# A diagonal LSTM and a small quantum circuit: late statistics in pieces of columns, state tiles reused as row buffers, new rows' states set by Pool

## The chip, the cores and the metric

One NeuronCore of one Trainium2 chip. The metric is device time in microseconds of the one core, and the time of a kernel is the median of its runs. A profile is of one execution; times inside it are in microseconds from the first instruction.

## The reference

The input `x` is 16 images of 128 channels, 64 rows and 64 columns, in float32. Two layers follow each other, each with a group norm ahead of it (32 groups of 4 channels) and a residual sum behind it.

Layer 0 is a diagonal LSTM. Row r is shifted right by r columns, so that 127 steps run over diagonals; a step takes all 64 rows at once:

```
i_s = w_is @ skew(gn(x)) + b_is
gates = i_s[t] + w_ss0 @ (h of the row above) + w_ss1 @ h + b_ss
o, f, i = sigmoid(gates[:384]);  g = tanh(gates[384:])
c = f * c + i * g;   h = o * tanh(c)
x1 = x + unskew(h)
```

A row's state also moves ahead of its first column: outside the image the input is zero, and the state that a row has reached when its first column comes depends on the row alone, not on the image.

Layer 1 works on each pixel: `gn(x1)` is projected to 4 angles, a fixed circuit of 4 qubits is simulated, its 4 expectation values are projected back to 128 channels, and `x1` is added. The group norm between the layers needs mean and variance of every group over all rows and columns of `x1`, so layer 1 can start only when the last column of the last row is there.

## The kernel before

**Tiling.** Channels are the 128 partitions. The 64 rows run in two bands of 32 slots. Slot s holds row s in band 0 and row 32 + s in band 1, which starts 65 steps later (`BAND`), so there are 160 steps (`NSTEP`). A step's columns are 16 images for each active slot, kept as two halves q (even and odd slots), up to 256 columns each. The window of active columns grows over the first 32 steps, is full to about step 128, and shrinks to the end (`columns`, `active`).

**Memory.** `ring` holds 40 of the 64 rows of all images; it is where x is read and where x1 is written. When a block of 4 rows of rows 0 to 23 is finished, SP writes it to a DRAM buffer `low` and loads rows 40 to 63 in its place. `spare` are four buffers of 512 columns. `hst` are two state buffers (read in one step, written in the next), `xns` two buffers of normalised input; both come from a pool of the scan.

**A step** (`step(t, ps)`, lines 736 to 844) is written out by hand for each engine, in program order:

- PE: products of the state with the recurrent weights into the gates' PSUM (line 745; with few columns `w1T` and `w0T` straight on the state, otherwise `wsT` on half 0, then both on differences), then the next step's input products (`gate_ps`, line 585).
- DVE: a difference of halves (line 604), `statistics(n)` (line 699), the sums of halves in PSUM for each gate (line 760), then `c * f` (806), `i * g` (812), the sum (815) and `h = tanh(c) * o` for each half (825).
- ACT: copies of a half (792), four gate activations (764), tanh (816).
- Pool: differences (607, 610), `residual(t - 1)`, which adds h to x in `ring` (619), `normalised(t + 2)` (566, 571, 576), and the group norm's late sums.

After line 825 come the states of rows that begin. `begin(copy, v, s, of, r)` copies row r's starting state, one column of `hinv` or `cinv`, to the 16 columns of slot s (line 600): for h on DVE, after the half q that the slot is in; for c on ACT. Starting states of rows from 33 on are computed inside the scan itself: in the first 32 steps one extra column rides behind the window (`reach`), and `waits` (line 721 on DVE; 727, 730 and 734 on Pool) moves it on.

**Statistics of the second group norm.** When the last row of a block of 4 rows is finished, `residual` puts (block, image) pairs into `waiting`, and each step takes 4 or 6 of them: `bn_stats` of 256 columns each, on DVE. Blocks 0 to 7 are summed in the middle of the scan (`early_sums`), which gives a provisional `mean2`. Each later block's deviations from it are added up on Pool as the block comes (`late_sums`). Four images of the last two blocks are instead summed on ACT (`by_scalar`, with `accum_out`). After the last step come the last residual, 12 `bn_stats` of the last block, 8 passes on ACT, the deviations, and a chain of small matmuls that sum over groups of channels (line 872), between which `fill` keeps PE busy. The mean and the variance lead to `rstd2` and to weights for each image.

**Layer 1** (lines 921 to 1054) runs over images: `angles` (950), `sines`, `squares` (978), `outputs` (996), `finish` (1013), which adds b and x1 and issues the store on SP (1015). Rows 0 to 23 of an image come back from `low` in three chunks, by Pool's DMA (`load`, line 848), through 14 buffers: the four `spare` and ten of a pool that takes the scan's memory. The four `spare` are loaded eight steps ahead of the scan's end, by SP; the other ten loads are issued after the scan.

## Time and profile before

| | |
|---|---|
| median of 3 runs | 1428.9 us (1428.24 to 1432.19) |
| profiled execution | 1429.22 us, span 1427.4 us |
| mean granted PE clock | 0.996 |
| PE busy | 1368.5 us (96%) |
| DVE busy | 973.7 us (68%) |
| ACT busy | 785.3 us (55%) |
| Pool busy | 903.7 us (63%) |
| moved by DMA | 107.05 MB |
| first gate activation | 105.9 us |
| last state written | 1285.1 us |
| first store issued | 1302.5 us |

A group's line of the profile reads: line, engine, operation, output<-input, shape, count, then busy time and length, and in brackets the engine's idle time ahead of it with what ended it. In the slices each digit is a fortieth of the span, in tenths busy. A busy PE is not PE at its peak: matmuls are pipelined and their ends are modelled. Times of Pool are rough.

### The profile page before, as it was taken

Reading aid. Unit: us, or ns where it says so; the run is one execution under the profiler, and the core shown is the slowest. Engines: PE = TensorE matmul, PEld = TensorE weight load, DVE = VectorE, ACT = ScalarE, POOL = GpSimd, SP = SyncE. Lnnn points to the kernel's source line nnn. Section 1 sums busy time; section 2 is a strip of 40 time slices with the busy share of each in tenths; the row PEclk is TensorE's granted clock in tenths of the full one; section 3 lists DMA queues with packets and bytes.
Section 4 is the critical chain, followed back from the end, with each engine's and each line's share of the span. In section 5 each row is a group of like instructions: output and inputs, shape, how many; then the busy total and the mean of one; then the engine's idle time right before and its main releaser. Section 6 shows DMA issues by size and latency. Waiting matters only on the chain. (4 is left out here: it accounts for less than half of the span.)

```text
span 1427.4 us, 20012 instructions
## 1 busy us (share of the span) xinstructions
PE 1368.5 (96%) x5984; PEld 967.6 (68%) x5984; DVE 973.7 (68%) x2438; ACT 785.3 (55%) x1888; POOL 903.7 (63%) x1747
## 2 busy tenths in 40 slices
PE   6778999999999999999999999999999999988898
PEld 5658887777766777667667777766777777883232
DVE  7984566566665666887777776555555578777877
ACT  4555666555555555555555555555555566555231
POOL 3225777777766677788878877766666667642120
PEclk9999999999999999999999999999999999999999
DMA  9970000000000000133333100000000000106999
GB/s 325 369 275 1 1 1 1 1 0 1 1 0 1 1 0 1 60 118 119 118 118 118 60 1 1 1 1 0 1 1 1 1 1 1 31 2 217 359 365 326
DMA packets 87756, 107.05 MB, mean 75 GB/s; under 512 B 5424, under 2 KB 72016, under 8 KB 87648
## 3 DMA queue, kind: packets, MB, share of 16 engines
q1 hardware_dynamic: 82688, 93.34, 19.1%
q0 software_dynamic: 3728, 11.62, 2.5%
q8 instruction: 48, 0.79, 0.2%
q10 hardware_dynamic: 1232, 0.80, 0.2%
q14 instruction: 60, 0.49, 0.1%
HBM read 59.61 MB, written 46.14 MB: 74 GB/s over the span
## 5 line engine op out<-in xcount | busy, mean ns | idle before, releaser
L585 PE MATMUL ps<-xn,wxT 128*128 128x512 f32 (+18 forms) x1280 | 481.3, 519 | 1.7 <-POOL xn L576 1.7
L760 DVE TENSOR_TENSOR ps<-ps,both 128x256 f32<-128x256 f32 (+9 forms) x544 | 221.1, 408 | 315.4 <-PE ps L745 306.2
L764 ACT ACTIVATE ps<-ps,bias 128x512 f32<-128x512 f32 (+23 forms) x480 | 279.2, 583 | 220.8 <-DVE ps L760 184.6
L585 PEld LDWEIGHTS ps<-xn,wxT 128*128 128x128 f32 x1280 | 232.5, 192 | 174.2 <-issue 155.5
L745 PE MATMUL ps<-spare,w1T 128*128 128x256 f32 (+14 forms) x1088 | 305.5, 362 | 0.0
L745 PE MATMUL ps<-spare,w0T 128*128 128x256 f32 (+14 forms) x1088 | 305.5, 362 | 0.0
L792 ACT COPY both<-ps 128x256 f32<-128x256 f32 (+9 forms) x544 | 191.6, 355 | 178.3 <-PE ps L745 158.8
L619 POOL TENSOR_TENSOR ring<-ring,hst 128x256 f32<-128x256 f32 (+8 forms) x488 | 247.9, 540 | 21.0 <-DVE hst L825 21.0
L745 PEld LDWEIGHTS ps<-hst,wsT 128*128 128x128 f32 x1088 | 195.8, 190 | 85.6 <-DVE hst L825 36.7
L745 PE MATMUL ps<-hst,wsT 128*128 128x256 f32 (+14 forms) x1088 | 241.4, 365 | 5.4 <-DVE hst L825 4.1
L745 PEld LDWEIGHTS ps<-spare,w0T 128*128 128x128 f32 x1088 | 201.1, 190 | 21.2
L745 PEld LDWEIGHTS ps<-spare,w1T 128*128 128x128 f32 x1088 | 201.0, 190 | 21.1
L576 POOL TENSOR_TENSOR xn<-xn,rstd 128x512 f32<-128x512 f32 (+10 forms) x160 | 170.8, 1067 | 12.5
L571 POOL TENSOR_TENSOR xn<-ring 128x256 f32<-128x256 f32 (+8 forms) x213 | 147.0, 700 | 0.0
L825 DVE TENSOR_TENSOR hst<-g,ps 128x256 f32<-128x256 f32 (+13 forms) x320 | 107.8, 368 | 45.2 <-ACT g L816 42.7
L816 ACT ACTIVATE g<-cst 128x256 f32<-128x256 f32 (+20 forms) x320 | 103.0, 368 | 64.3 <-DVE cst L815 63.5
L566 POOL TENSOR_TENSOR xn<-ring,mean 128x16 f32<-128x16 f32 (+8 forms) x247 | 130.9, 540 | 7.5 <-DVE mean L143 6.1
L610 POOL TENSOR_TENSOR spare<-hst 128x240 f32<-128x240 f32 (+9 forms) x136 | 103.1, 758 | 35.5 <-DVE hst L825 31.6
L764 ACT ACTIVATE g<-ps,bias 128x512 f32<-128x512 f32 (+20 forms) x160 | 97.3, 608 | 28.4 <-DVE ps L760 22.2
L843 POOL COPY spare<-hst 128x16 f32<-128x16 f32 x64 | 25.1, 392 | 134.2 <-DVE hst L825 134.2
L815 DVE TENSOR_TENSOR cst<-cst,ps 128x256 f32<-128x256 f32 (+20 forms) x320 | 104.4, 368 | 5.5
L812 DVE TENSOR_TENSOR ps<-ps,g 128x512 f32<-128x512 f32 (+20 forms) x160 | 95.1, 594 | 17.7 <-ACT g L764 17.3
(355 smaller groups left out, 1244.0 us busy)
## 6 DMA issues: line engine op xcount, KB each, us to landing
ring<-in_x_dram SPq DMA_DIRECT2D x80, 256.0 KB, 5.6
out_dram<-ring SPq DMA_DIRECT2D x80, 256.0 KB, 5.0
low<-ring SPq DMA_DIRECT2D x6, 2048.0 KB, 7.8
ring<-in_x_dram SPq DMA_DIRECT2D x6, 2048.0 KB, 8.0
low<-low POOLq DMA_DIRECT2D x32, 256.0 KB, 5.6
out_dram<-low SPq DMA_DIRECT2D x32, 256.0 KB, 5.0
spare<-in_x_dram SPq DMA_DIRECT2D x27, 256.0 KB, 5.5
rest<-in_x_dram SPq DMA_DIRECT2D x21, 256.0 KB, 5.6
```

Of the source, the lines that this page charges most:

```text
L566: nc.gpsimd.tensor_sub(by_pairs(xn, 0, j, n), x0, over(mean1, n))
L571: nc.gpsimd.tensor_sub(by_pairs(xn, 1, j, n), lower, of)
L576: nc.gpsimd.tensor_mul(v, v, r)
L585: nc.tensor.matmul(ps[g][:, :, a:b], lhsT=wxT[:, g * 128 : (g + 1) * 128], rhs=xns[t % 2][:, :, a:b], start=t > 0, stop=True, skip_group_c ...
L610: nc.gpsimd.tensor_sub(diff[:, 0, a1:b], now[:, 1, a1 - NB : b - NB], now[:, 0, a1:b])
L619: nc.gpsimd.tensor_add(x1, x1, by_pairs(new, q, j, n))
L745: nc.tensor.matmul(out, lhsT=w[:, g * 128 : (g + 1) * 128], rhs=rhs, start=False, stop=True, skip_group_check=True,)
L760: nc.vector.tensor_add(v, v, both[g][:, a:b])
L764: nc.scalar.activation(to[:, :, a:w], ps[g][:, :, a:w], FUNC[g], bias=bias[:, g : g + 1])
L792: nc.scalar.copy(both[g][:, a:b], ps[g][:, 0, a:b])
L815: nc.vector.tensor_add(c[:, q], c[:, q], ig[:, q])
L825: nc.vector.tensor_mul(new[:, q, a:v], th[:, q, a:v], act[GO][:, q, a:v])
```

## The change

1. **Statistics by pieces.** Blocks 8 to 13 are taken in two halves of columns (0 to 31, 32 to 63), each as soon as it is finished in all four rows; block 14 in 48 and 16 columns; block 15 in 48 and 12 columns. `statistics` takes a budget in microseconds of estimated work (0.12 plus 0.0035 a column) where it took a count. Pieces' deviations are scaled by the piece's share, one more instruction on Pool for each, and `late_sums` runs for each piece.
2. **A last strip.** The last 4 columns of block 15, all images at once, are done after the last step: a subtraction of `mean2`, a square and two sums. The passes on ACT (`by_scalar`) and the DVE deviations of the last block go. In the last three steps a second call of `statistics` stands ahead of the last gate's sum. Two fills fewer stand among the matmuls.
3. **State tiles.** `xns` and `hst` are now `spare` 4 to 7. At the scan's end SP loads low rows 4, 5 and 7 into them in the last two steps, and row buffer 6 after the last residual. The pool of other low buffers has six instead of ten.
4. **New rows' states.** In band 0 a new row's h is copied by Pool, early in the step, not by DVE at its end, and the multiplication of the odd half leaves these columns out where they are its last. In band 1 the copy stays on DVE, behind both halves. `waits` writes both halves' extra column with one instruction.
5. **Fills of the sums.** `added` and `inner` are zeroed and `by_one` is made at step 32 rather than ahead of step 0; `sums_of` and `less` go.

The changed kernel's order on the engines, where the diff alone does not tell it: on Pool, two runs of `late_sums` and the issue of the first load of the pool's six buffers stand ahead of the last residual. The numbers of pieces by step are 9 and 7 in steps 101 and 102, and so on every four steps to 122; 9, 7 in 133, 134 and 137, 138; then 9, 8, 7, 5, 6, 7, 6 in steps 141 to 147, 5 to 7 in steps 148 to 155, none in 156, and 11, 11 and 10 in the last three.

The diff, cut to its core:

```diff
-    spare = [const.tile([P, CHUNK], F32, name=f"spare{i}") for i in range(4)]
+    spare = [const.tile([P, CHUNK], F32, name=f"spare{i}") for i in range(8)]
...
-        hst = [state.tile([P, 2, NC], F32, name=f"hst{i}") for i in range(2)]
-        xns = [state.tile([P, 2, NC], F32, name=f"xn{i}") for i in range(2)]
+        xns, hst = ([v.rearrange("p (q n) -> p q n", q=2) for v in spare[i : i + 2]] for i in (4, 6))
...
-                if t == 4 * g + 3 + (NW - 1 if 4 * g < SLOTS else BAND + NW - 1 - SLOTS):
-                    n = NB - LATE if g >= NG2 - 2 else NB
-                    waiting.extend((g, i) for i in range(n))
+                done = t - (4 * g + 3 + (-1 if 4 * g < SLOTS else BAND - 1 - SLOTS))
+                ends = pieces(g)
+                if done in ends:
+                    k = ends.index(done)
+                    w0 = ends[k - 1] if k else 0
+                    waiting.extend((g, k, w0, done, i) for i in range(NB))
...
-        for v in (added, inner, sums_of):
-            nc.gpsimd.memset(v, 0.0)
-        nc.gpsimd.tensor_scalar_mul(by_one, group, 1.0 / (NG2 * BLOCK))
+        def prepared():
+            for v in (added, inner):
+                nc.gpsimd.memset(v, 0.0)
+            nc.gpsimd.tensor_scalar_mul(by_one, group, 1.0 / (NG2 * BLOCK))
...
+        def pieces(g):
+            if g < FIRST:
+                return (NW,)
+            if g == NG2 - 1:
+                return (3 * NW // 4, NW - STRIP)
+            return (NW // 2, NW) if g < NG2 - 2 else (3 * NW // 4, NW)
+
+        def late_sums(g, k, share):
+            e = 2 * (g - FIRST * k)
+            m = mean2.unsqueeze(2).to_broadcast([P, NB, 2])
+            nc.gpsimd.tensor_sub(dev[:, 0], parts[:, :, e : e + 2, 1], m)
+            nc.gpsimd.tensor_mul(dev[:, 1], dev[:, 0], dev[:, 0])
+            nc.gpsimd.tensor_scalar_mul(dev, dev, share)
+            nc.gpsimd.tensor_add(added, added, dev)
+            nc.gpsimd.tensor_add(inner, inner, parts[:, :, e : e + 2, 2])
             yield
...
-        def statistics(n):
-            for _ in range(min(len(waiting), n)):
-                g, i = waiting.pop(0)
+        def statistics(us):
+            while waiting:
+                g, k, w0, w1, i = waiting[0]
+                us -= 0.12 + (w1 - w0) * 0.0035
+                if us < 0.0:
+                    break
+                waiting.pop(0)
...
-                nc.vector.bn_stats(stats[:, i, g, :], ring[:, q, i, :])
+                v = ring[:, q, i, :].rearrange("p (r w) -> p r w", w=NW)[:, :, w0:w1]
...
+                nc.vector.bn_stats(stats[:, i, g - FIRST * k, :], v)
...
             if to < NC:
-                for k in range(q + 1):
-                    if k != q or to > v:
-                        state(new[:, k, to : to + 1])
+                if q or to > v:
+                    state(new[:, 0 : q + 1, to : to + 1])
...
+            if t + 1 < SLOTS:
+                begin(nc.gpsimd.tensor_copy, new, t + 1, hinv, t + 1)
             ready, sums[:] = list(sums), []
-            statistics(4 if w - a <= LEAST else 6)
+            statistics(1.65 if w - a <= LEAST else 2.1)
...
+            if t > NSTEP - 4:
+                statistics(0.4)
             add(GO)
...
             for q in range(2):
-                v = w if q == few and columns(t + 1)[1] == b else b
-                nc.vector.tensor_mul(new[:, q, a:v], th[:, q, a:v], act[GO][:, q, a:v])
+                v = w if q == few == 0 and columns(t + 1)[1] == b else b
+                if q == 1 and t + 1 < SLOTS and t % 2 == 0:
+                    v = b - NB
+                if a < v:
+                    nc.vector.tensor_mul(new[:, q, a:v], th[:, q, a:v], act[GO][:, q, a:v])
                 if q == few and w > b:
                     waits(t, b, th, act[GO], new)
-                for s, r in fresh:
-                    if s % 2 == q:
-                        begin(nc.vector.tensor_copy, new, s, hinv, r)
-                        begin(nc.scalar.copy, cst, s, cinv, r)
+            s = t + 1
+            if s < SLOTS:
+                begin(nc.scalar.copy, cst, s, cinv, s)
+            s -= BAND
+            if 0 <= s < SLOTS:
+                begin(nc.vector.tensor_copy, new, s, hinv, SLOTS + s)
+                begin(nc.scalar.copy, cst, s, cinv, SLOTS + s)
...
+            if t == SLOTS:
+                prepared()
...
-            if t >= NSTEP - LATE:
-                by_scalar(NG2 - 2, NB - NSTEP + t)
-            if t == NSTEP - 8:
-                for n in range(4):
-                    low_rows(nc.sync, n, spare[n])
+            for n in {NSTEP - 8: range(4), NSTEP - 2: (4,), NSTEP - 1: (5, 7)}.get(t, ()):
+                low_rows(nc.sync, n, spare[n])
...
-            residual(NSTEP - 1, hst[NSTEP % 2])
+            statistics(10.0)
             for later in sums:
                 for _ in later:
                     pass
-            g, n = NG2 - 1, NB - LATE
-            for i in range(n, NB):
-                by_scalar(g, i)
+            residual(NSTEP - 1, hst[NSTEP % 2])
+            low_rows(nc.sync, 6, spare[6])
...
-            for _ in range(3):
-                fill()
-            statistics(len(waiting))
-            deviations(nc.vector, g, n)
-            for h in range(2):
-                add(ps[:, 1, 0:n], by_one, parts[:, 0:n, 2 * g + h, 2])
-            add(ps, by_one, sums_of[:, 1])
-            for h in range(2):
-                add(ps[:, :, 0:n], by_half, dev[:, :, 0:n, h])
+            fill()
+            v = ring[:, block(NH - ROWS)].rearrange("p i (r w) -> p i r w", w=NW)[:, :, :, NW - STRIP :]
+            d, sq = (work.tile([P, NB, ROWS, STRIP], F32, name=f"strip{i}", tag=f"both{i}") for i in range(2))
+            m = mean2.unsqueeze(2).unsqueeze(3).to_broadcast([P, NB, ROWS, STRIP])
+            nc.vector.tensor_sub(d, v, m)
+            nc.vector.tensor_mul(sq, d, d)
+            for i, u in enumerate((d, sq)):
+                u = u.rearrange("p i r w -> p i (r w)")
+                nc.vector.reduce_sum(strip_sums[:, i], u, axis=mybir.AxisListType.X)
+            add(ps, by_one, strip_sums)
...
-    lowp = ctx.enter_context(tc.tile_pool(name="lowp", bufs=10))
+    lowp = ctx.enter_context(tc.tile_pool(name="lowp", bufs=6))
...
-        lows[n] = spare[n % NBUF] if n % NBUF < 4 else lowp.tile([P, CHUNK], F32, name=f"low{n}", tag="low")
-        if n >= 4:
+        lows[n] = spare[n % NBUF] if n % NBUF < 8 else lowp.tile([P, CHUNK], F32, name=f"low{n}", tag="low")
+        if n >= 8:
             low_rows(nc.gpsimd, n, lows[n])
```

## The prediction

> **What bounds the kernel now.** I read the page's slices first, then a table of stretches, then the time line around each place that the diff touches.
>
> ```profile
> PE   6778999999999999999999999999999999988898
> DMA  9970000000000000133333100000000000106999
> ...
> 209.00:574.00 365.00, 365.00 (x1388) 261.94 (x1387) 235.01 (x591) 210.64 (x444) 260.64 (x384) 1.00 0.00 1
> 660.00:1120.00 460.00, 460.00 (x1708) 323.98 (x1707) 294.65 (x715) 264.20 (x556) 336.76 (x544) 1.00 0.11 36
> 1302.50:1427.40 124.90, 113.96 (x538) 37.52 (x536) 99.54 (x155) 34.62 (x58) 18.23 (x34) 0.97 0.98 341
> ```
>
> The columns of the last three lines are the stretch, its length, busy us of PE, PEld, DVE, ACT and POOL, the granted clock, the DMA share and GB/s. There are five regimes. Loads and first statistics (to 105.9 us) are DMA's. From about step 21 (209 us) to step 128 (1120 us) PE is busy without a gap, 8.61 us a step: what other engines save there is worth nothing, and what makes PE wait is lost for good. In the ramp before it (steps 0 to 20) and in the run-out after it a step is a chain PE, ACT, DVE and back. From 1282 to 1302.5 us runs the serial stretch from the last step to the first store. The store phase (1302.5 to the end) moves data at 98% of the DMA engines and only shifts with its start. So gains can lie in the start, the ramp, the run-out and the serial stretch.
>
> **The serial stretch.** Time line at its start (start, length, engine, line):
>
> ```profile
> 1284.85 0.29 DVE L825 TENSOR_TENSOR hst<-g,ps 128x16 f32<-128x16 f32 x2 [0.32 <-issue]
> 1285.22 0.23 POOL L619 TENSOR_TENSOR ring<-ring,hst 128x16 f32<-128x16 f32 x1 [2.81 <-DVE hst L825]
> 1285.48 4.02 DVE L699 BATCH_NORM_STATS2 stats<-ring 128x6 f32<-128x256 f32 x12 [0.34 <-POOL ring L619]
> ...
> 1291.39 0.17 DVE L890 COPY m<-gm 128x16 f32<-128x16 f32 x1 [1.38 <-PE gm L872]
> ```
>
> The last state is there at 1285.14, and 6.25 us later the mean goes on: residual, 12 statistics of whole blocks, deviations, matmuls queued behind three fills. The 12 statistics, the 16 ACT passes and the deviations go. In their place stand a subtraction, a product and two sums of 128x256 on DVE. Such a product takes 0.42 us here and starts 0.34 (or, dependent, 0.45) after the one before; a sum of 128x256 took 0.49 (line 652): 0.45 + 0.36 + 0.45 + 0.49 = 1.75. Then a matmul pair and its hand-over, 0.5.
>
> What the diff hides is Pool's queue. The built order puts two groups of five instructions (`late_sums`) and the first low-row load, a DMA issued by Pool, ahead of the last residual. Four such instructions ran from 1276.78 to 1277.95 (1.17 us); the fifth, on 64 columns, makes about 1.5 a group. Pool is free at 1282.40, so the groups end at 1285.4; ten issues took 5.40, so one is 0.54, and the residual 0.23: it ends near 1286.3 instead of 1285.45. Its load waits for ACT's last use of the weights' space, at 1284.44, done by then. So m comes at 1286.3 + 0.06 + 1.75 + 0.5 = 1288.6, 2.8 us earlier; I take **2.7**. Ends: 3.8 if Pool is not late, 1.2 if runs of four elements (no row shows such) double the strip's cost. The Sqrt table load (1.28 us) moves into ACT's idle time ahead of it. PE's single remaining fill (1.1 us) fits the strip's time.
>
> The loads into the states' tiles are worth nothing by this trace: 14 buffers stay, 34 loads follow the first store as before, and DMA is only 0.52 busy from 1299 to 1302.5, so the ten early loads were out of the way. On SP the four loads stand ahead of the stores; the last of them waits for Pool's residual at 1286.3, and nothing is behind it on SP until the first store, over 10 us later. ACT's passes beside steps 156 to 159 ended ahead of the next gate (1276.38 against 1276.49), so there their removal gives nothing.
>
> **Start.**
>
> ```profile
> 103.42 0.17 DVE L153 SCALAR_TENSOR_TENSOR rstd<-sq,r 128x16 f32<-128x16 f32 x1
> 103.79 0.15 POOL L643 MEMSET added<- 128x64 f32 x1 [2.34 <-DVE rstd L153]
> ...
> 104.15 0.53 POOL L645 TENSOR_SCALAR by_one<-wide_sb 128x128 f32<-128x128 f32 x1
> 104.76 0.25 POOL L576 TENSOR_TENSOR xn<-xn,rstd 128x32 f32<-128x32 f32 x1
> ...
> 105.07 3.68 PE L585 MATMUL ps<-xn,wxT 128*128 128x128 f32 x16 [1.67 <-POOL xn L576]
> ```
>
> Three fills and a product stand on Pool between rstd (103.59) and the first xn, which PE waits for. They go to step 32, where Pool has over 2 us a step free (68% busy). xn then starts at 103.65 to 103.85: **1.05** gained (0.9 to 1.1). PE ran these matmuls at a granted clock of 0.50 (105.1 to 108.5), after a window of 3.4 us in which it was busy 1.60; an earlier start makes that window 2.7 busy. At full clock 8 such matmuls take 1.06 instead of 1.84, of which the first gate's quarter and the pace of the next is on the path: 0 to 0.5, taken as **0.2**. [...]
>
> **Ramp.** What PE waits for at the end of steps 0 and 1:
>
> ```profile
> 107.92 0.28 DVE L825 TENSOR_TENSOR hst<-g,ps 128x16 f32<-128x16 f32 x2 [0.28 <-ACT g L816]
> ...
> 108.12 0.15 DVE L721 TENSOR_TENSOR hst<-g,ps 128x1 f32<-128x1 f32 x1
> 108.24 0.17 DVE L600 COPY hst<-hinv 128x16 f32<-128x16 f32 x1
> ...
> 108.46 0.32 PEld L745 LDWEIGHTS ps<-hst,w1T 128*128 128x128 f32 x2
> ...
> 111.46 0.21 DVE L721 TENSOR_TENSOR hst<-g,ps 128x1 f32<-128x1 f32 x2
> ```
>
> In even steps 2 to 10 the copy of the new row's state is last on DVE; on Pool, early in the step, it leaves the one-column product last: 0.14 less, five times 0.70 (step 0 gains 0.05, as PE is still busy there). In odd steps 1 to 11 two one-column products (0.21) become one (0.15) and the copy no longer stands ahead of the second half: 0.06 + 0.04, six times 0.6. In steps 13, 15, 17, 19 the copy follows the first half; without it PE goes 0.08 sooner, four times 0.3. Sum **1.6**; ends 0.7 (ACT or Pool sets some of these steps) and 2.2. Pool pays 31 copies of 0.20; it idles 1.1 to 1.8 us a step here waiting for DVE, and the next xn has a step of slack. Without that cover the 0.2 would fall on each step's difference for PE, 6 us in all.
>
> **Second band.** Here the copy stays on DVE but moves behind both halves:
>
> ```profile
> 774.75 0.42 DVE L825 TENSOR_TENSOR hst<-g,ps 128x256 f32<-128x256 f32 x1 [0.28 <-ACT g L816]
> ...
> 775.21 0.17 DVE L600 COPY hst<-hinv 128x16 f32<-128x16 f32 x1
> 775.29 0.41 DVE L825 TENSOR_TENSOR hst<-g,ps 128x256 f32<-128x256 f32 x1
> 775.75 1.89 PE L745 MATMUL ps<-hst,wsT 128*128 128x256 f32 x8
> ```
>
> PE's first product needs an even row's copy. It will end at 775.71 (as in odd steps, 0.04 before PE's start) instead of 775.38; PE starts 0.055 after what it waits for, so it loses 0.015. Where DVE is already late (steps 68 and 72, PE idle 0.38 behind that copy) it loses 0.33. 14 x 0.015 + 2 x 0.33 = **-0.9**. Ends: -0.2 and, all 16 late, -5.3.
>
> **Pieces.** Durations of one statistic, smallest, median and largest in ns:
>
> ```profile
> L285 DVE BATCH_NORM_STATS2 stats<-rest x21: 693/694/695, 15.9 to 97.2; 128x6 f32<-128x512 f32 x21
> L699 DVE BATCH_NORM_STATS2 stats<-ring x248: 401/409/428, 596.1 to 1289.1; 128x6 f32<-128x256 f32 x124
> ```
>
> By their slope 128 elements take 0.267, and less the overlap of neighbours (12 in 4.02 are 0.33 apart) 0.185; 192 take 0.26. In steps 101 to 122 nine and seven pieces are new: 1.7 and 1.3 us. At 879 to 882 us DVE has 2.73 between the difference and the first gate's sum, 0.41 of it a sum of means: covered. The five Pool instructions behind each piece (1.5 us) fit Pool's idle 2 us. In the run-out that gap is 1.5 us at 160 columns (step 140) and about 1.15 at 128. Six whole statistics (1.96) overran it in steps 138, 141 and 142, by 1.3 in all, and four (1.30) by 0.15 in each of steps 145 to 147. After, steps 141 to 146 have 1.75, 1.62, 1.82, 1.30, 1.36 and 1.36: 1.5 over. Net **0.1**, ends -0.8 and 0.8. [...]
>
> **Sum.** 2.7 + 1.05 + 0.2 + 1.6 - 0.9 + 0.1 = 4.75 us. The profiled execution took 1429.22 us (span 1427.4 and 1.8 around it), 0.3 above the median of 1428.9. From the median: **1424.2 us**, with an own range of 1422 to 1426.5.
>
> **Rivals.** (1) No change, 1426 to 1429: the end gains only 1.2 (slow strip, late Pool) and the second band loses 3 or more because DVE runs 0.35 late, as it does in steps 88, 108 and 116. For it: PE is saturated there and no loss is made good. Against: 12 of 16 even steps stand exactly on time. (2) Slower, 1432 to 1448: a piece costs what a whole statistic costs. At 0.33 us nine take 2.9 and seven 2.3; the run-out's gaps are overrun by 9 instead of 1.7, the net is +3 us; at 0.41, without overlap, +19. It decides from 0.29 a piece, where the gain is used up. For it: the pieces are four short runs with gaps, which no row shows. Against: the slope between 256 and 512. (3) More, 1421: the four loads ahead (1.05 MB at 341 GB/s, 3.1 us) do shorten the store phase. Against: DMA's idle half before the first store.
>
> **Numbers.** The forecast has 0.55, rival 1 0.21, rival 2 0.12, rival 3 0.12. A measurement of this kernel tells 0.3% from no change, 4.3 us: below 1424.6 is faster, above 1433.2 slower. Of the forecast 0.46 lies below 1424.6; with rival 3, faster 0.58. Slower 0.10 (rival 2 but for 0.02), the same 0.32. The range 1421 to 1429.5 leaves out rival 2 and the edges.
>
> **What would show it.** Right: first gate activation near 104.8; step 21 some 2.7 us earlier than before; pieces 0.19 apart; from the last state to the mean 3.5 us instead of 6.25; store phase 124.9. Wrong: pieces at 0.3 or more; PE idle in every second step from 568 to 836; a store phase that changes by over 2 us; Pool's residual after 1.5 us behind the last state.

## The result, and the profile after

| | before | after |
|---|---|---|
| median, first set | 1428.75 us (7 runs, 1426.6 to 1432.19) | 1424.76 us (7 runs, 1422.2 to 1425.63) |
| ratio, first set | | 0.9964, 95% interval 0.9949 to 0.9978 |
| median, second set | 1427.87 us (20 runs) | 1425.9 us (11 runs) |
| ratio, second set | | 0.999, 95% interval 0.9979 to 1.0001 |
| profiled execution | 1429.22 us, span 1427.4 | 1422.99 us, span 1421.1 |

So the change makes the kernel some 2 to 4 us faster by the medians, 0.1 to 0.4%; the second set's interval reaches no change at all. The two profiled spans differ by 6.3 us, more than the medians do, and the first question is how much of that is the change. I cut every profiled execution at the same events. Three stretches come out: the loads up to the end of the first group norm (rstd on DVE), the computed stretch from there to the first store, and the store phase.

| profiled span, us | before | after | after, second execution |
|---|---|---|---|
| loads, to the end of rstd | 103.59 | 102.93 | 104.00 |
| rstd to the first product of step 1 | 4.99 | 3.12 | 3.70 |
| step 1 to step 21 | 91.29 | 90.54 | 90.54 |
| step 21 to step 65 | 368.01 | 368.00 | 368.00 |
| step 65 to step 131 | 569.10 | 569.57 | 569.54 |
| step 131 to step 159 | 145.10 | 145.70 | 145.70 |
| step 159 to the last state | 3.05 | 3.05 | 3.06 |
| last state to the mean | 6.25 | 3.98 | 3.98 |
| mean to the first product of the angles | 2.11 | 3.34 | 3.19 |
| that product to the first store | 8.98 | 8.98 | 8.99 |
| sum, rstd to first store | 1198.89 | 1196.28 | 1196.70 |
| store phase | 124.92 | 121.88 | 122.63 |

The computed stretch repeats to a few hundredths of a microsecond wherever the clock does the same; loads and store phase differ from execution to execution. In the computed stretch the change gained 2.61 us in the first pair of profiles. The other 3.7 of the 6.3 lie in the loads (0.66), which the change does not touch, and in the store phase (3.04), of which more below.

The page's slices of the kernel after show the same five regimes:

```profile
PE   6778999999999999999999999999999999888998
DMA  9970000000000000133333100000000000005999
```

The table of stretches of the kernel after (columns as before: stretch, length, PE, PEld, DVE, ACT, POOL, granted clock, DMA share, GB/s) has two lines from the last stretch that have no fellow in the profile before, and the store phase:

```profile
1282.87:1286.28 3.41, 2.07 (x11) 1.24 (x11) 1.55 (x5) 1.27 (x2) 3.08 (x8) 1.00 0.52 171
1286.28:1289.69 3.41, 3.41 (x6) 1.54 (x6) 2.05 (x11) 1.70 (x3) 0.93 (x2) 0.50 1.01 343
1299.21:1421.10 121.89, 112.39 (x538) 37.93 (x536) 99.57 (x155) 34.62 (x58) 18.52 (x34) 0.98 0.99 349
```

PE ran at half clock from 1286.28 to 1289.69. The store phase moved 349 GB/s at a DMA share of 0.99, against 341 at 0.98 before.

**The serial stretch**, time line of the kernel after (start, length, engine, line; line numbers are of the changed kernel):

```profile
1282.62 0.29 DVE L835 TENSOR_TENSOR spare<-g,ps 128x16 f32<-128x16 f32 x2 [0.31 <-POOL dev L686]
...
1283.69 0.65 POOL L860 DMA_DIRECT2D low<-low  x1 [0.30 <-POOL inner L689]
...
1284.36 0.24 POOL L618 TENSOR_TENSOR ring<-ring,spare 128x16 f32<-128x16 f32 x1
...
1284.64 0.42 DVE L894 TENSOR_TENSOR strip<-ring,mean 128x256 f32<-128x256 f32 x1 [1.73 <-POOL ring L618]
...
1286.67 2.06 PE L183 MATMUL I-10725_10726<-w_amp,w_out 128*128 128x512 f32 x2
1286.89 0.17 DVE L902 COPY m<-gm 128x16 f32<-128x16 f32 x1 [0.72 <-PE gm L883]
...
1290.23 0.71 PE L962 MATMUL theta<-ring,w_image 128*32 128x512 f32 x2
```

The last state is there at 1282.91. Pool is then still in its late sums, issues a load (0.65 us), and only then does the last residual, which ends at 1284.60. DVE's strip waits 1.73 us for it. The mean goes on at 1286.89, 3.98 us after the last state instead of 6.25. But the fill at 1286.67 takes 2.06 us where the same fill took 1.02 to 1.10 before, and the angles start at 1290.23, 3.34 us behind the mean instead of 2.11.

**The start**, time line of the kernel after:

```profile
102.75 0.18 DVE L153 SCALAR_TENSOR_TENSOR rstd<-sq,r 128x16 f32<-128x16 f32 x1
...
103.08 0.25 POOL L575 TENSOR_TENSOR spare<-spare,rstd 128x32 f32<-128x32 f32 x1 [2.29 <-DVE rstd L153]
...
103.38 2.05 PE L584 MATMUL ps<-spare,wxT 128*128 128x128 f32 x16 [0.65 <-POOL spare L575]
```

Pool's first multiplication is recorded 0.15 us behind rstd (102.93), not 1.17, so 1.02 us sooner, and the sixteen first products take 2.05 us instead of 3.68: no window of half clock fell on them here.

**The second band**, time line of the kernel after at the first of the two steps where PE was already late:

```profile
598.97 0.76 DVE L835 TENSOR_TENSOR spare<-g,ps 128x256 f32<-128x256 f32 x2 [0.28 <-ACT g L829]
...
599.64 0.17 DVE L599 COPY spare<-hinv 128x16 f32<-128x16 f32 x1
...
599.86 0.92 PE L753 MATMUL ps<-spare,wsT 128*128 128x256 f32 x3 [0.59 <-DVE spare L599]
```

The copy now stands behind both halves, and PE idles 0.59 us for it. In the profile before, the same bracket had 0.38:

```profile
602.89 0.92 PE L745 MATMUL ps<-hst,wsT 128*128 128x256 f32 x3 [0.38 <-DVE hst L600]
```

**The pieces**, the answer for the line of the statistics in the kernel after (durations in ns, smallest, median, largest):

```profile
L706 DVE BATCH_NORM_STATS2 stats<-ring x384: 192/280/422, 592.9 to 1280.7; 128x6 f32<-128x128 f32 x96, 128x6 f32<-128x256 f32 x64, 128x6 f32<-128x192 f32 x16, 128x6 f32<-128x64 f32 x8
...
  POOL ring L618: 21.0, 18
```

The second line stands under "who waited for it": Pool's residual waited 18 times, 21.0 us in all, for the statistics. In the profile before only one weight load of PE waited for them (0.2 us).

### The profile page after: what moved, and what is told of

Its sections match the earlier page's. It is cut to its first block, busy times and chain, and to the rows that moved or that the text cites. A ratio compares the mean times of both kernels' runs of the same rounds, so it can differ in the third digit from the quotient of the medians.

```text
span 1421.1 us, 20142 instructions
## 1 busy us (share of the span) xinstructions
PE 1364.6 (96%) x5970; PEld 964.5 (68%) x5970; DVE 981.4 (69%) x2538; ACT 778.0 (55%) x1856; POOL 921.9 (65%) x1824
## 5 line engine op out<-in xcount | busy, mean ns | idle before, releaser
L584 PE MATMUL ps<-spare,wxT 128*128 128x512 f32 (+18 forms) x1280 | 479.6, 518 | 0.7 <-POOL spare L575 0.7
L753 PE MATMUL ps<-spare,w1T 128*128 128x256 f32 (+16 forms) x1272 | 345.8, 353 | 9.9 <-DVE spare L835 4.9
L584 PEld LDWEIGHTS ps<-spare,wxT 128*128 128x128 f32 x1280 | 230.9, 190 | 173.2 <-issue 155.5
L753 PE MATMUL ps<-spare,w0T 128*128 128x256 f32 (+16 forms) x1272 | 343.8, 352 | 0.8 <-POOL spare L609 0.8
L618 POOL TENSOR_TENSOR ring<-ring,spare 128x256 f32<-128x256 f32 (+8 forms) x488 | 248.1, 540 | 31.2 <-DVE stats L706 21.0
L753 PEld LDWEIGHTS ps<-spare,wsT 128*128 128x128 f32 x1088 | 194.8, 190 | 86.4 <-DVE spare L835 34.7
L753 PE MATMUL ps<-spare,wsT 128*128 128x256 f32 (+14 forms) x1088 | 241.3, 365 | 5.4 <-DVE spare L835 3.7
L575 POOL TENSOR_TENSOR spare<-spare,rstd 128x512 f32<-128x512 f32 (+10 forms) x160 | 171.0, 1069 | 14.8 <-DVE rstd L153 2.3
L570 POOL TENSOR_TENSOR spare<-ring 128x256 f32<-128x256 f32 (+8 forms) x213 | 147.5, 703 | 0.0
L565 POOL TENSOR_TENSOR spare<-ring,mean 128x16 f32<-128x16 f32 (+8 forms) x247 | 131.3, 541 | 5.8 <-DVE mean L143 5.6
```

Source lines behind the costliest of these rows:

```text
L565: nc.gpsimd.tensor_sub(by_pairs(xn, 0, j, n), x0, over(mean1, n))
L570: nc.gpsimd.tensor_sub(by_pairs(xn, 1, j, n), lower, of)
L575: nc.gpsimd.tensor_mul(v, v, r)
L584: nc.tensor.matmul(ps[g][:, :, a:b], lhsT=wxT[:, g * 128 : (g + 1) * 128], rhs=xns[t % 2][:, :, a:b], start=t > 0, stop=True, skip_group_c ...
L618: nc.gpsimd.tensor_add(x1, x1, by_pairs(new, q, j, n))
L753: nc.tensor.matmul(out, lhsT=w[:, g * 128 : (g + 1) * 128], rhs=rhs, start=False, stop=True, skip_group_check=True,)
```

## Experiments

Each kernel was timed beside the kernel before, whose median was 1427.87 to 1429.33 us in the sets, and each left one profile. Since a whole time spreads by 2.5 to 10 us over the runs of one kernel, verdicts rest on stretches of the profile.

| kernel | median, us (runs) | ratio to before, 95% interval | rstd to first store | last state to mean | mean to angles |
|---|---|---|---|---|---|
| after, again | 1425.9 (11) | 0.999, 0.9979 to 1.0001 | 1196.70 | 3.98 | 3.19 |
| row buffers by Pool | 1422.39 (5) | 0.9964, 0.995 to 0.9978 | 1193.78 | 2.73 | 2.11 |
| two fills | 1424.15 (9) | 0.9969, 0.9957 to 0.998 | 1194.78 | 3.75 | 2.11 |
| sums first | 1423.2 (6) | 0.9967, 0.9956 to 0.9978 | 1194.54 | 3.20 | 3.42 |
| start alone | 1427.81 (12) | 0.9986, 0.9975 to 0.9997 | 1199.65 | 7.94 | 2.11 |
| copy between | 1425.93 (10) | 0.9973, 0.9961 to 0.9985 | 1197.10 | 3.98 | 3.64 |
| copies on DVE | 1427.69 (12) | 0.9986, 0.9972 to 1.0001 | 1196.10 | 3.77 | 3.32 |
| all three mends | 1421.77 (6) | 0.9951, 0.9938 to 0.9963 | 1193.44 | 2.39 | 3.56 |
| best | 1421.02 (6) | 0.9947, 0.9932 to 0.9962 | 1191.89 | 2.38 | 2.10 |
| small products | 1424.22 (11) | 0.9971, 0.9959 to 0.9982 | 1196.16 | 3.98 | 3.28 |
| before, again | 1430.3 (12) | 1.0007, 0.9994 to 1.0019 | 1202.66 | 9.59 | 2.11 |
| own tiles | 1423.42 (5) | 0.9965, 0.9951 to 0.9979 | 1194.89 | 3.54 | 2.52 |

**The changed kernel again.** No edit.

> The changed kernel once more, as the measure for the other runs of this set. The two profiled executions differ by 6.3 us of span, the medians by 4.0: of the 6.3, 0.66 lie ahead of the scan (end of the first group norm at 102.93 against 103.59) and 3.0 in the store phase (121.9 against 124.9), places that the statistics and the states do not touch. Theory A (a store phase differs from one execution to the next): this execution's store phase lies anywhere from 121.5 to 125 us, and its end differs from the first one's by as much, while the stretch from the end of the first group norm to the first store repeats within 0.1 us (1196.3). Theory B (the loads ahead of the scan's end make the store phase shorter): 121.9 again within 0.5.

Store phase 122.63, 0.75 longer than the first time; loads 1.07 longer; computed stretch 0.42 longer: 0.58 more in the start and 0.15 less behind the mean, the two places where the clock fell. Theory A holds for the store phase. Its claim of a computed stretch within 0.1 us does not: the window of half clock moves.

**Row buffers 4 to 7 loaded by Pool, after the scan.**

```diff
-            for n in {NSTEP - 8: range(4), NSTEP - 2: (4,), NSTEP - 1: (5, 7)}.get(t, ()):
+            for n in {NSTEP - 8: range(4)}.get(t, ()):
...
-            low_rows(nc.sync, 6, spare[6])
...
-        if n >= 8:
+        if n >= 4:
...
-        for n in range(NBUF):
+        for n in (0, 1, 2, 3, 6, 4, 5, *range(7, NBUF)):
             load(n)
```

> The changed kernel with row buffers 4 to 7 loaded by Pool after the last residual, behind no step of the scan, as the ten were before; nothing else differs but that Pool issues the load of row buffer 6 first, behind the last residual. Theory A (the early loads are worth nothing, the store phase only shifts): time within 1 us of the changed kernel's; the last residual is 0.65 us earlier at least, as no load's issue stands ahead of it. Theory B (the prediction's rival 3, that the loads ahead shorten the store phase): store phase back at 124.9, time 2 to 3 us above the changed kernel's.

Store phase 122.68, as with the early loads, and the time is not longer but shorter, 1422.39 us against 1425.9 for the changed kernel in the same set: theory B, the prediction's rival 3, falls. The reason for the gain is in the first place a side effect: the first load now needs the last state's tile, so it can no longer be issued ahead of the last residual. The residual ends 0.65 us behind the last state instead of 1.69, and the mean comes 2.73 us behind it instead of 3.98. That is 1.25 us. The other 1.23 of the 2.50 us of computed stretch is the clock, which stays up between mean and angles. This half is not shown to belong to the loads: without early loads, but with tiles of their own (the last run below), the clock fell. The early loads brought the store phase nothing.

**A second fill.**

```diff
-            fill()
+            for _ in range(2):
+                fill()
```

> The changed kernel with a second fill ahead of the strip's sums (three before the change, one after it). In the changed kernel PE ran at a granted clock of 0.51 from 1286.2 to 1289.6, after 3.4 us in which it was busy 2.02, and the first product of the angles came 3.31 us behind the mean, against 2.08 before. Theory (the missing fill lets the clock fall): with it the clock stays at 1.0 there, the mean comes at the same place (3.9 to 4.1 us behind the last state), the first product of the angles 2.1 us behind the mean, and the first store 1.2 us earlier. Rival (PE waits for something else, such as the sine table's load on ACT, which ends at 1289.24): no gain, and the fill delays the mean by up to 0.3.

Two stretches of the last stage of this kernel:

```profile
1282.27:1285.68 3.41, 2.30 (x12) 1.57 (x12) 1.35 (x7) 1.91 (x5) 2.91 (x8) 1.00 0.35 103
1285.68:1289.10 3.42, 2.96 (x12) 1.10 (x14) 2.40 (x13) 1.62 (x3) 1.66 (x4) 1.00 0.98 344
```

The clock stays at 1.00, the angles come 2.11 us behind the mean, and the mean is even 0.23 earlier: from the last state to the first store 14.84 instead of 16.30. The earlier mean is the clock too: in the four executions of changed kernels whose clock was full up to the mean, this one among them, it comes 2.07 to 2.08 us behind the residual's end, and in the kernel after 2.29. The theory holds; in this execution one of the two fills that the change took out is worth 1.46 us.

**Late sums ahead of the residual in each step.** The loop over `ready` moves from behind `normalised(t + 2)` to ahead of `residual(t - 1, now)`.

> The changed kernel with the late sums ahead of Pool's residual in each step, instead of behind the next input. In the changed kernel step 144 lost 0.95 us: Pool's residual of step 142 waited 1.36 us for the seven statistics of the same block, so the five instructions of the late sums ran from 1219.03 to 1220.81, past the end of the step, and the difference that PE waits for came 1.4 us late. Theory: the late sums fill Pool's wait instead; from step 143 to step 145 the lead over the kernel before no longer falls by 1.07 but by less than 0.2, and the time is 0.9 us lower. Rival (the seven statistics themselves are the loss, on DVE): the lead falls by 0.8 or more as before and the time is the same.

In the changed kernel, time line of steps 143 and 144:

```profile
1216.03 1.18 POOL L618 TENSOR_TENSOR ring<-ring,spare 128x128 f32<-128x128 f32 x3 [1.36 <-DVE stats L706]
...
1219.03 0.26 POOL L685 TENSOR_TENSOR dev<-stats,mean 128x32 f32<-128x32 f32 x1
...
1220.76 0.45 POOL L609 TENSOR_TENSOR spare<-spare 128x128 f32<-128x128 f32 x1
...
1221.27 0.49 PE L753 MATMUL ps<-spare,w0T 128*128 128x128 f32 x2 [0.75 <-POOL spare L609]
```

The last state of step 143 is there at 1219.29, but Pool starts the difference (line 609) at 1220.76, behind the five late sums, and PE waits. With the late sums ahead, Pool's time line at the same step (0.94 us later on the clock of this execution):

```profile
1216.98 1.35 POOL L618 TENSOR_TENSOR ring<-ring,spare 128x16 f32<-128x16 f32 x4
...
1220.31 0.56 POOL L609 TENSOR_TENSOR spare<-spare 128x128 f32<-128x128 f32 x1
```

The difference starts 0.08 us behind the last state (1220.23). From step 143 to step 145 it took 10.49 us instead of 11.51; steps 131 to 159 took 144.68 instead of 145.70, less than the 145.10 of before. The same seven and five pieces ran on DVE, so the rival falls: the pieces' DVE time is covered, and what cost step 144 was Pool's queue. The last residual came 0.7 us earlier too, which had not been expected.

**The start alone**, on the kernel before.

```diff
-        for v in (added, inner, sums_of):
-            nc.gpsimd.memset(v, 0.0)
-        nc.gpsimd.tensor_scalar_mul(by_one, group, 1.0 / (NG2 * BLOCK))
+        def prepared():   # the same three lines, called at t == SLOTS
```

> The kernel before the change, with only the fills of the sums and the product for the group matrix moved from ahead of step 0 to step 32. Theory: from the end of the first group norm to the first product of step 1 the time falls from 4.99 us to 3.1, if the window of half clock does not fall there (as in three of four profiled executions of changed kernels), or to 3.7 if it does (as in the fourth); 1.14 of it is the wait of the first input, the rest clock. The stretch from there to the first store stays at 1193.9 us as before the change, and the store phase anywhere from 121.5 to 125. Rival (the clock's part does not belong to these fills): 3.85. Whole time 1.3 to 1.9 us below the kernel before.

3.87 us from rstd to step 1: 1.12 gained, and a window of half clock on the first products (102.61 to 106.03), so nearer to the rival's 3.85 than to 3.7. But 3.7 came from the second profile after, where Pool copies the new row's state; here DVE still does it at the end of step 0, which costs 0.13 (3.25 against 3.12 in the run with the copies on DVE, neither with a slow window there). With that the theory has 3.83, and the run does not tell it from the rival. The stretch behind it was 1195.78, 1.88 longer than before (1193.90): 0.14 in the ramp and 1.69 between the last state and the mean, where the clock fell from 1287.04 to 1290.45 in a kernel whose fills were those of before.

**The second band's copy between the halves**, as before the change.

```diff
                 if q == few and w > b:
                     waits(t, b, th, act[GO], new)
+                s = t + 1 - BAND
+                if 0 <= s < SLOTS and s % 2 == q:
+                    begin(nc.vector.tensor_copy, new, s, hinv, SLOTS + s)
...
-                begin(nc.vector.tensor_copy, new, s, hinv, SLOTS + s)
```

> The changed kernel with the second band's copy of a new row's state between the two halves again, as before the change. The second band took 569.10 us from step 65 to step 131 before, 569.54 to 569.57 in four profiled executions since. Theory (the copy behind both halves delays the odd half's multiplication for PE, and it is paid in steps 65, 68 and 72 alone): 569.10 again, 0.45 less, not the 0.9 that the prediction charged. Rival (the pieces or the Pool instructions cost it): 569.55.

569.09 us from step 65 to step 131: the theory, to the hundredth. The longer computed stretch (1197.10) is the clock: it was 0.5 from 1284.49 to 1291.32 and again from 1298.15 to 1301.56, and from the first product of the angles to the first store it took 10.02 us, not 8.98.

**The first band's copies on DVE again.** The copy returns behind the half of its slot, and the odd half is multiplied whole.

> The changed kernel with the first band's copies of the new rows' states on DVE again, behind the half that the slot is in, and the odd half's multiplication whole; the joint writing of the two halves' extra column stays. The ramp from step 1 to step 21 took 91.29 us before, 90.54 since. Theory (in steps 1 to 11 PE waits for DVE's last instruction, so the copy's place sets it; from step 12 on it does not): 91.1 to 91.2, as 0.06 in each of six odd steps is the joint writing's and the rest the copy's. Rival (the joint writing alone made the gain): 90.6. Rival 2 (the prediction's price of 1.6 for the ramp, 1.2 of it in steps 12 to 20): over 91.5.

91.09 us: 0.55 of the ramp's 0.75 is the copy's, 0.20 the joint writing's. A second thing came that nobody had expected: the run-out took 145.06 us, not 145.70. Steps 134, 135 and 147 take 18.97 or 18.98 us together here and in the three executions of kernels with the old copies, 19.62 to 19.64 in the ten whose copies are Pool's. In step 134 of the kernel after, the state's product on DVE starts 0.45 us behind the end of the tanh that it needs, here 0.09; no row shows what DVE does in between. No copy of the first band stands in these steps, so why its place matters there stays open. (Rival 2 misquotes the prediction, which charged 0.3, not 1.2, to the steps after 12.)

**All three mends together**: row buffers by Pool, late sums first, copy between.

> The changed kernel with three mends: row buffers 4 to 7 loaded by Pool behind the last residual; the late sums ahead of the residual in each step; the second band's copy between the halves. Theory (each mend is worth alone what it is worth together): from the end of the first group norm to the first store 1193.8 (row buffers by Pool) - 1.02 (late sums) - 0.45 (copy) = 1192.3 us, against 1196.3 in the changed kernel and 1198.9 before; time 3.9 us below the changed kernel's, 6 to 7 below the kernel before. Rival (the late sums' earlier place takes from Pool what the last residual gained, or the clock falls in the last stretch): 1193.5 or more.

1193.44, near the rival's bound: the last residual now ends 0.31 us behind the last state and the mean 2.39, so the mends do add up, but the clock fell (1285.74 to 1289.16) and took 1.45 back between mean and angles.

**Best: the same with a half fill.**

```diff
             add(ps, by_half, moments, True)
+            half_fill()        # one product of 256 columns into a spare PSUM buffer
             for h in range(2):
```

> The kernel with the three mends, and a half fill (one product of 256 columns, 0.5 us) between the product of the moments and those of the late sums, where PE sat idle for 0.49 us. With the three mends alone the first product of the angles came 3.56 us behind the mean, as the granted clock was 0.5 from 1285.74 to 1289.16. In the ten profiled executions so far, a window of 3.41 us was followed by a slow one wherever its matmuls streamed columns for 1.41 us or less (at 1.0 ns a column and pass: a fill of 512 columns is two passes of 0.51), and by no slow one from 1.5 us on, in the first load phase and in the last stretch; in the kernel with the three mends that window streamed 1.41. Theory (the clock goes by streamed columns): the half fill brings it to 1.9, the clock stays at 1.0, angles 2.11 behind the mean, from the end of the first group norm to the first store 1192.0 us instead of 1193.44, time 1.4 us below the kernel with the three mends. Rival (the half fill delays the late sums' products and the mean, or the clock falls all the same): 1193.2 or more.

```profile
1282.17:1285.58 3.41, 3.12 (x10) 1.16 (x9) 2.42 (x11) 1.62 (x4) 3.32 (x7) 1.00 0.57 179
1285.58:1289.00 3.42, 3.08 (x27) 1.15 (x30) 1.08 (x6) 1.01 (x3) 2.08 (x4) 1.00 0.87 309
```

The clock stays at 1.00, angles 2.10 behind the mean, computed stretch 1191.89: the sum that was expected, to 0.1 us. At 1421.02 us it beats the kernel before by 0.4 to 0.7% and, by medians of different sets, the changed one by 3.7 to 4.9 us.

**Small products.**

```diff
             fill()
+            small_ps = ps_gate.tile([P, 512], F32, name=nc.get_next_instruction_name(), tag="gate")
+            for _ in range(5):
+                nc.tensor.matmul(small_ps[:, 0:16], lhsT=w_out, rhs=w_amp[:, 0, 0:16], start=True, stop=True)
```

> The changed kernel with five products of 16 columns (ten passes at a pitch of 0.11 us, as the others of this size have) behind its one fill ahead of the strip: PE is busy for 1.1 us more in that stretch by the profile, as with the second fill, but streams only 0.16 us of columns more. Theory (streamed columns set the clock): the slow window stays, and the first product of the angles comes 3.2 to 3.6 us behind the mean, as in the changed kernel. Rival (the busy share of PE sets it): 2.1 us, as with the second fill, and the first store 1.2 us earlier.

```profile
1282.81:1286.22 3.41, 2.93 (x20) 2.45 (x20) 1.67 (x6) 1.40 (x2) 3.00 (x9) 1.00 0.54 157
1286.22:1289.64 3.42, 3.42 (x8) 1.62 (x7) 2.06 (x12) 1.70 (x3) 1.03 (x2) 0.50 0.97 344
```

A window in which PE was busy 2.93 of 3.41 us is followed by one of half clock, while with two fills one of 2.30 was not. Busy time does not set the clock; streamed columns fit every case ahead of the angles.

**The kernel before again.** No edit.

> The kernel before, for its store phase. Two profiled executions with the loads as before the change had 124.92 and 124.19 us from the first store to the end; eight with changed buffers 121.88 to 124.47, mean 123.0. Theory A (one population, the store phase differs from execution to execution): this one anywhere from 121.5 to 124. Theory B (the change made the store phase 1.5 us shorter, by other means than the early loads): 124.2 to 125. From the end of the first group norm to the first store 1198.9 us, unless the clock falls in the last stretch (1200.5).

Store phase 124.50, which theory B had (what the runs say of it together stands in the next section). The computed stretch is 1202.66: two windows of half clock in a row (1288.40 to 1295.23) made the stretch from the last state to the mean 9.59 us instead of 6.25. The profile on which the prediction was made was a lucky one in this place. Its window around the last state, in which PE was busy 1.59 us against 1.33 here, was followed by full clock:

```profile
1282.69:1286.10 3.41, 1.59 (x15) 1.48 (x14) 2.10 (x11) 2.68 (x12) 0.72 (x4) 1.00 0.00 0
```

**Own tiles.** The change without its third part: `hst` and `xns` in their own pool, four `spare`, ten buffers of the pool, loads by Pool as before. (Its expectation says nine early loads fewer; it is four.)

> The changed kernel without its third part: the states and the normalised input have tiles of their own again, four spare buffers and ten of the pool, nine loads fewer ahead of the scan's end and all ten by Pool behind the last residual. Three profiled executions with these buffers had 124.19 to 124.92 us from the first store to the end (mean 124.5), ten with eight spare and six of the pool 121.88 to 124.47 (mean 123.0), whether the early loads were there or not. Theory A (which buffers are which sets the store phase): 124 to 125, time as the changed kernel's or higher although the last stretch is shorter. Theory B (something else in the change, or chance): 121.9 to 123.5. In both the last residual comes within 0.7 us of the last state, as no load stands ahead of it, and from the end of the first group norm to the first store it takes 1193.8 us, if the clock does not fall in the last stretch, as in the kernel with the row buffers loaded by Pool.

Store phase 122.69: theory A falls, the choice of buffers does not set it. The residual comes 0.66 us behind the last state, so it was the third part of the change that let a load be issued ahead of it. The clock fell from 1285.60 to 1289.02 and kept the computed stretch at 1194.89.

## Why the prediction was right, and where its steps were not

The forecast held: 1424.2 us for 1424.76 (1425.9 in the second set), inside the range, and faster was the likelier side. Its sum did not hold as well. In the computed stretch it had 4.75 us, and the profiles after show 2.61 and 2.19; in the profiled pairs the rest lies in the store phase, on which no change was forecast, and in the loads. So the direction rests on mechanisms that were right, while the closeness of the total is in part luck.

| term | predicted | measured | |
|---|---|---|---|
| start (xn behind rstd) | 1.05 | 1.02 | right |
| clock at the start | 0.2 (0 to 0.5) | 0.72 and 0.14 | mis-sized: it falls or not |
| ramp | 1.6 (0.7 to 2.2) | 0.75, and 0.13 in step 0 | mis-sized |
| second band | -0.9 (-5.3 to -0.2) | -0.47 | mis-sized |
| run-out | 0.1 (-0.8 to 0.8) | -0.60 | Pool's cover failed; 0.65 open |
| end, to the mean | 2.7 (1.2 to 3.8) | 2.27 | residual 0.53 later |
| end, mean to angles | 0 | -1.23 and -1.08 | missed |
| store phase | 0 | 3.04 and 2.29 in the pairs | a slow window in the profile before |

- **Start.** The wait was read rightly; by the rows it is 1.02 (Pool's start 0.15 instead of 1.17 behind rstd), not the 1.14 that the start's own experiment expected. Of the rest, 0.13 is the copy in step 0, which the prediction put at 0.05. The clock's part was charged to the first gate only; without the slow window 0.32 come up to the first activation and 0.40 more in the rest of step 0. Where the window did fall on these products, as in the second profile after, 0.14 is left.
- **Ramp.** The mechanism was right (DVE's last instruction sets steps 1 to 11), the sizes were not: by the lead at each step, even steps 2 to 10 gained 0.49 in all (0.70 predicted), odd steps 0.15 (0.60), all later ones 0.11 (0.30). From step 12 on PE hardly waits for the copy (0.03 in each even step in the run that puts it back); that part was read off the order on DVE alone.
- **Second band.** Steps 68 and 72 lost 0.22 and 0.19, not 0.33 each, one more step 0.05, the other 13 nothing: 0.015 a step was charged to a copy that ends before PE asks for it. Rival 1, which needed 3 us or more here, fell with it.
- **Pieces.** By start to start, 128 elements cost 0.193 us (0.185 predicted) and 192 cost 0.260 (0.26). Rival 2 needed 0.29. A single piece lasts 0.280 in the trace; the next one starts 0.193 behind it, and that is what a row of them costs.
- **Run-out.** The step that failed is "The five Pool instructions behind each piece (1.5 us) fit Pool's idle 2 us." They are queued behind the residual, and the residual waits for the pieces. The statistics now read blocks that are still being written, so Pool's residual waits until the pieces are read, 1.36 us in step 143; that wait was not in the prediction, although the change adds it. The run with the late sums first shows it: without this the run-out gains 0.42. Another 0.65 went in steps 134, 135 and 147, as the run with the copies on DVE shows, where the prediction had no loss; its cause is open. Without these two losses the run-out would have gained 1.07, where the prediction had 0.1 net.
- **End.** The late residual was foreseen, its time not: two groups of late sums took 3.27 us (3.0 predicted), the load 0.65 (0.54), and 0.30 went by idle. From the residual's end to the mean it was 2.29 for 2.31 predicted, a little by luck, as 0.22 of it is the slow clock. Missed was the price of the fills. The prediction said that one fill "fits the strip's time" and did not ask what the clock does when the others go, although it had the same fall at the start in its own rows.
- **Store phase.** Rival 3 held that the early loads shorten it. They do not (122.68 without them), nor does the choice of buffers (122.69). What parts the 14 executions is a window of half clock in or at the edge of the store phase, ahead of PE's last product (behind it the clock is 0.5 in the profiles before and after alike, from 1422.65 and 1415.98 us). Five have one and took 124.08 to 124.92 us: both of the kernel before and the start alone, but also the run with the late sums first and the one with the copy between. The nine without took 121.88 to 123.30. The means are 1.73 apart, about half a window. In the run with the late sums first:

```profile
1387.97:1391.38 3.41, 3.41 (x12) 0.56 (x12) 0.22 (x1) 0.00 (x0) 0.54 (x1) 0.50 1.05 390
```

  In four of the five, PE stood idle 1.3 to 2.4 us for the load of a low row just ahead of the window. Such a wait alone does not make the phase long: with own tiles there were three over 1.1 us and no slow window, and it took 122.69. No kernel was made to test it, so that the clock causes the 1.7 us is argued, not shown. Whether the change makes such a window rarer (these three of three, two of the other eleven) is open.

In the comparison of medians a part of the gain is likely the clock in the kernel before: its last stretch lost 3.34 us in its second profiled execution and 1.69 in that of the start alone, where this stretch is the same, and nothing in the one that was at hand for the prediction.

## What to carry to other kernels

Ask of each queue what stands behind the instruction that will wait: here the work that was added to Pool was small, but it stood between a new wait and the one difference that PE needed, and moving it ahead of the wait gave 1.02 us for nothing. A filler matmul is a term of the sum like any other: before it is taken out, add up the columns that remain in each 3.41 us, wherever such a window may begin (here 1.45 us of them was followed by half clock, 1.54 was not). And cut several executions at the same events before a difference of spans is explained: over the 14 executions the loads vary by 2.05 us and the store phase by 3.04, as much as the change is worth.

## What the runs showed of the hardware

- **Ahead of layer 1 the clock goes by streamed columns.** For each matmul its columns were counted at 1.0 ns each and pass (a fill of 512 columns is two passes of 0.51 us), up to 0.06 us ahead of its record's end, and added up in the windows of 3.41 us on the grid that the clock's own steps mark. From 94 to 112 us and from 1270 us to the first product of the angles, 14 profiled executions have 147 windows at full clock. The 14 with 1.45 us or less of columns were each followed by a window at half clock, none of the 133 with 1.54 or more was. By busy time there is no such line: 2.93 busy was followed by half clock, 1.59 was not. Ten of the executions gave the rule, two kernels were then made to test it, and the last two fell in line. In layer 1 the line does not hold: there five windows with 2.9 to 4.1 us by the same count were followed by half clock. The matmuls there have forms such as 128*32 and 32*128 instead of 128*128; how they count is open. Ahead of PE's last product the slow stretches of these executions are 3.41 us long, or two in a row (6.83), and their place differs between executions of one kernel: in the first of the kernel before the clock was half from 105.10 and from 1330.49 us and full from 1286.10 to 1289.52, in the second it was half from 1288.40. The window ahead of one need not be idle: 1.45 us of columns, 42% of its length, was already too little.
- **A lucky window hides a cost.** The same last stretch took 6.25, 7.94 and 9.59 us in the kernel before, the start alone and the kernel before again, with none, one and two windows at half clock. By the count above one can estimate, from the matmuls of an execution, for how many places of the grid some window there holds 1.45 us or less: 70% in the kernel before, 45% with the row buffers by Pool and 32% with two fills, all three of which were spared, and none in the best kernel, where no window holds under 1.92. So a single profile with full clock proves a fill only if the count holds for every place of the grid.
- **Pool's issue of a load** took 0.54 us in a row of ten in the kernel before, but 0.65 alone behind other Pool work in the kernel after, with 0.30 of idle time ahead of it.
